# Row maxima turned by VectorE in four blocks, instead of by TensorE through PSUM

## The chip, the cores and the metric

One NeuronCore of a Trainium2 chip. The metric is the device time of one execution in microseconds; lower is better. Engines are named as in the profile: PE is TensorE (PEld its weight load), DVE is VectorE, ACT is ScalarE, POOL is GpSimd, SP is the engine whose queue issues nearly all DMAs.

## What is computed

One block of a diffusion transformer in float32: 16 batches of 256 tokens, width 256, 16 heads of 16. Self-attention with modulation and a gate, cross-attention to a context of 256 tokens, then an MLP of width 1024.

```python
x_norm = modulate(_ln(x), shift_a, scale_a)
q, k, v = split(x_norm @ W_qkv + b_qkv)
attn_w = softmax(einsum('bhqd,bhkd->bhqk', q, k) * scale)
x = x + gate_a[:, None] * (attn_out @ W_proj + b_proj)
q_c, (k_c, v_c) = _ln(x) @ W_qc + b_qc, split(_ln(context) @ W_kvc + b_kvc)
x = x + cross_attention(q_c, k_c, v_c) @ W_cproj + b_cproj
h = gelu(modulate(_ln(x), shift_m, scale_m) @ W_mlp1 + b_mlp1) @ W_mlp2 + b_mlp2
x = x + gate_m[:, None] * h
```

The softmax is taken against the exact maximum of each row of scores.

## The kernel before

The two attentions of 16 batches are 32 *units* n = 0 to 31, each one attention of one batch: s0 to s4, then alternating s5, c0, s6, c1 up to s15, c10, then c11 to c15 (s: self, c: cross). While unit n is computed, units ahead of it are prepared: n+1 has its scores for the maxima (`s`), n+2 its projections Q, K, V, n+3 its transposed, normalised input, n+4 its statistics. What is one step in the order of work for n is therefore mostly work of other units. In the loop, an even unit n from 2 to 22 has a self-attention unit at n+3 and a cross-attention unit at n+4; an odd one from 3 to 21 the other way round; from n = 23 on all that lie ahead are cross-attention.

Each unit has eight *beats* k = 0 to 7 (`beat(n, k)`). All engines and SP keep the program's order. In a beat, `visit(n, k)` first puts on PE four matmuls `s` (scores of unit n+1, rows on the partitions) and four matmuls `st` (scores of unit n, turned, with the negative maximum added through a 64th row of the operand). `s` has one PSUM buffer, which DVE reduces into `mx` (TENSOR_REDUCE) before the next beat's `s` may write it; `st` has one, which ACT turns into probabilities `pt` (`exp`) before the next `st`. After that each beat has its share of the rest: `o` (attention times values, `av_part`) in even beats, projections of n+2 and n+3 (`lanes`) in odd ones, input transposes (`psT`).

Q and K are kept in a stack `big` of 2 x 63 rows: high part, low part, high part (`h_q`, `l_q` and so on, sent by DMA from the projections), and in rows 63 and 127 the row maxima against a row of ones. `m_part(u, hf)` makes these rows for half `hf` of the heads: half 0 is complete after beat 3 of the unit before and used from beat 0 of unit u, half 1 complete after beat 7 and used from beat 4. PE transposes the 16 columns of `mx` into PSUM (`psm`), ACT negates them into `m`, SP sends `m` to the two rows. Half 0 stands in beat 4, half 1 in beat 0 of the unit itself.

Other names: `transposed(...).high` and `.low` make the high part `xTh` (ACT) and the remainder `xTl` (DVE for self-attention, in two pieces; for cross-attention ACT copies `y` and POOL subtracts) from one PSUM tile `psT`, in beat 3. `ln[0].steps[0]` are the statistics of a layer norm (`st_s`, `st_c`, DVE), `steps[1]` the aggregates `mv` and POOL's power `rs`, `steps[2]` POOL's application `xn`. For the attention's denominators, `pull` fetches sums `S` and outputs `U`, `recip` inverts S on DVE, `spread` writes S to DRAM (`rd`), `back` reads it back spread out as `R` (in beat 5), `norm` multiplies on POOL. The MLP follows the units and is not touched.

Of the kernel before, what the change touches and what calls it, by code (L numbers as in the profile page):

```python
# [21 lines left out]
def pixart_block(  # L22
# [56 lines left out]
    DVE.memset(wz, 0.0)  # L79
    ident = const.tile([P, P], F32, name="ident")  # L80
    make_identity(nc, ident)
    mhalf = const.tile([P, 2], F32, name="mhalf")
    POOL.memset(mhalf, -0.5)

# [1 line left out]
    vts = [const.tile([P, NT, NH, 32], F32, name=f"v{i}") for i in range(3)]  # L86
    wself = const.tile([P, 16, H], F32R, name="wself")
    ones = const.tile([8, N], F32, name="ones")
    DVE.memset(ones, 1.0)


    BMOD, BQKV, BQC, BKVC, BM1 = 0, 12, 18, 20, 24
# [246 lines left out]
    def transposed(src, name, scale=None, pool=False):  # L339

        o = Box()

        def place():
            o.ps = ps_gen(f"psT_{name}", SHORT)

        def turn(fs=range(KC)):
            if len(fs) == KC:
                place()
            for f in fs:
                for t in range(NT):  # L350
                    PE.transpose(o.ps[:, f * N + t * P:f * N + (t + 1) * P],
                                 src()[:, t, f * P:(f + 1) * P], ident)

        def high():
            hi = work.tile([P, KC, N], F32R, tag="xTh", name=f"xTh_{name}", bufs=4)
            lo = work.tile([P, KC, N], F32R, tag="xTl", name=f"xTl_{name}", bufs=4)
            o.xT = (hi, lo)
            if scale is None:
                ACT.copy(hi.rearrange("p k n -> p (k n)"), o.ps)
            else:  # L360
                for f in range(KC):
                    ACT.activation(hi[:, f], o.ps[:, f * N:(f + 1) * N], AF.Identity, scale=scale[f])

        def low():
            hi, lo = o.xT
            if scale is None:
                DVE.tensor_tensor(lo.rearrange("p k n -> p (k n)"), o.ps,
                                  hi.rearrange("p k n -> p (k n)"), ALU.subtract)
            else:
                for f in range(KC):  # L370
                    DVE.scalar_tensor_tensor(lo[:, f], o.ps[:, f * N:(f + 1) * N], scale[f],
                                             hi[:, f], ALU.mult, ALU.subtract)

        def full():
            o.y = work.tile([P, KC, N], F32, tag="y", name=f"y_{name}", bufs=1)
            if scale is None:
                ACT.copy(o.y.rearrange("p k n -> p (k n)"), o.ps)
            else:
                for f in range(KC):
                    ACT.activation(o.y[:, f], o.ps[:, f * N:(f + 1) * N], AF.Identity, scale=scale[f])  # L380

        def rest_pool():
            hi, lo = o.xT
            POOL.tensor_tensor(lo, o.y, hi, ALU.subtract)

        def low_pool():
            full()
            rest_pool()

        o.full, o.rest_pool, o.place = full, rest_pool, place  # L390
        o.parts = [turn, high, low]
        o.low_pool = low_pool
        o.turn, o.high, o.low = turn, high, low_pool if pool else low
        return o
# [245 lines left out]
    def s_tile(u, g, par, t, bank=None, home=sp):  # L640

        alone = bank is None
        if alone:
            turn_of_s[0] ^= 1
            bank = turn_of_s[0]
        apart = isinstance(home, tuple)
        for j in range(2):
            PE.matmul((home[bank] if apart else home[:, bank])[:, j * N:(j + 1) * N],  # L650
                      u.q[par * 64:par * 64 + 63, 2 * g + j, t * P:(t + 1) * P],
                      u.k[par * 64:par * 64 + 63, 2 * g + j, :], start=True, stop=True)
            if j == 0:
                yield
        if u.mx is None:
            u.mx = work.tile([P, 2, 2, 4, NT], F32, tag="mx", name=f"mx_{u.n}", bufs=3)
        mx = u.mx.rearrange("p f r a t -> p r f a t")
        a = slice(2 * (g % 2), 2 * (g % 2) + 2)
        if alone or apart:
            src = home[bank] if apart else sp[:, bank]  # L660
            DVE.tensor_reduce(mx[:, par, g // 2, a, t], src.rearrange("p (j n) -> p j n", j=2),
                              AX.X, ALU.max)
        elif bank == 1:
            DVE.tensor_reduce(mx[:, :, g // 2, a, t], home.rearrange("p r (j n) -> p r j n", j=2),
                              AX.X, ALU.max)
        yield

    def m_part(u, hf):

        pst = ps_gen(f"psm_{u.n}_{hf}", SHORT)  # L670
        PE.transpose(pst[:16, :P], u.mx[:, hf].rearrange("p r a t -> p (r a t)"), ident)
        m = work.tile([16, P], F32R, tag="m", name=f"m_{u.n}_{hf}", bufs=1)
        ACT.mul(m, pst[:16, :P], -1.0)
        SP.dma_start(u.q[63:P:64, 4 * hf:4 * hf + 4, :].bitcast(F32), m.bitcast(F32))

    def t_part(u, pair, par):

# [306 lines left out]
    def beat(n, k):  # L984
# [17 lines left out]
        if k == 4 and q2:  # L1002
            q2.Q.high()
            q2.Q.send_high()
        if k == 6:
            if q2 and not n:
                q2.V.keep()
            if p2 and not alone:
                p2.end()
        visit(n, k)  # L1010
        if k == 0:
            if cur:
                m_part(cur, 1)
            exps()
            if q3 and q3.ready:
                q3.T[0].place()
# [11 lines left out]
        elif k == 1:  # L1028
            exps()
            run(lanes(q2 and q2.Q, q2 and n and q2.V))  # L1030
            if prev:
                p1.pull(1)
            if lc:
                lc.ln[0].steps[0]()
            if lx:
                if lx.b in (0, B - 1):
                    lx.ln[1].steps[0]()
                lx.ln[1].steps[1]()
                lx.ln[1].steps[2]()
        elif k == 2:  # L1040
            exps()
            if cur:
                av_part(cur, 0)
            if q3:
                q3.T[0].turn((1,) if q3.ready else (0, 1))
            if ls:
                ls.ln[0].steps[0]()
            elif prev:
                p1.recip()
                p1.spread()  # L1050
            if not (q3 and q3.kind == "c"):
                spare(n)
        elif k == 3:
            if q3:
                q3.T[0].high()
                if q3.kind == "c":
                    q3.T[0].full()
            exps()
            if alone and p2:
                p2.proj(0)  # L1060
                p2.proj(1)
            elif n:
                run(lanes(p2, q2 and q2.Q))
            else:
                run(lanes(q2.V, q2.Q))
            if q3 and q3.kind == "s":
                q3.T[0].low()
            if prev and ls:
                p1.recip()
                p1.spread()  # L1070
        elif k == 4:
            if nxt and lx:
                m_part(nxt, 0)
            exps()
            if nxt and not lx:
                m_part(nxt, 0)
            if alone:
                p2.end()
            if cur:
                av_part(cur, 1)  # L1080
            if lx:
                lx.T[1].turn()
            if q2:
                q2.Q.low()
                q2.Q.send_low()
            if q3 and q3.kind == "c":
                q3.T[0].rest_pool()
                spare(n)
            if ls:
                ls.ln[0].steps[1]()  # L1090
                ls.ln[0].steps[2]()
                ls.ready = True
        elif k == 5:
            exps()
            run(lanes(q3 and q3.K, (None if alone else p2) if n else q2.V))
            if cur:
                o_out(cur, 0)
            if lc:
                lc.ln[0].steps[1]()
                lc.ln[0].steps[2]()  # L1100
                lc.ready = True
            v = unit(n + 5)
            if v and v.kind == "c":
                load(v)
            if prev:
                p1.back()
        elif k == 6:
            exps()
            if lx:
                lx.T[1].high()  # L1110
            if cur:
                cur.post.begin()
                av_part(cur, 2)
                cur.post.pull(0)
            if q3 and p2:
                q3.vk = lanes(q3.V, q3.K)
                run(q3.vk, 1)
            if p3:
                p3.store()
            if lx:  # L1120
                lx.T[1].full()
                lx.T[1].rest_pool()
        elif k == 7:
            exps()
            run(q3.vk if q3 and p2 else lanes(q3 and q3.V, q3 and q3.K))
            if late:
                p2.add()
                p2.added = True
            elif lc:
                lc.ln[1].steps[0]()  # L1130
            v = unit(n + 5)
            if v and v.kind == "s":
                load(v)
            if n == nu - 1:
                p2.add()
                p2.store()
# [99 lines left out]
```

## Time and profile before

| | |
|---|---|
| three runs | 748.71, 742.05, 743.37 us; median 743.37 |
| the profiled execution | 742.45 us, span of its trace 740.7 us |
| PE, DVE, ACT, POOL busy | 722.2, 569.4, 556.1, 528.5 us |
| granted clock of TensorE | 0.999 |
| DMA | 106.15 MB, mean 143 GB/s |

A row of a timeline gives the start in us from the span's beginning, the duration, the engine, the line (every operation goes through one helper, so all have L51), the operation, out<-in by the program's names, the shape, how many are merged (x4), and in brackets how long the engine was idle before it and what released it. SPq rows are DMAs being issued, not their transfer. A row of groups gives busy us, mean ns of one, and idle time before.

### The profile page before, as it was taken

How to read it: one execution, taken by the hardware profiler on the slowest of the kernel's cores; microseconds unless marked ns; L12 is line 12 of the kernel's file. 1: busy time of each engine (PE TensorE's matmuls, PEld its weight loads, DVE VectorE, ACT ScalarE, POOL GpSimd, SP SyncE). 2: the span in 40 equal slices, each digit the busy share in tenths (PEclk: the TensorE clock that was granted, in tenths of full speed). 3: DMA queues.
4: the chain of work that ended last, by engine and by line, in shares of the span. 5: the costliest groups of instructions: out<-in, count | busy, mean ns of one | idle time of the engine just before them, and what ended most of it. 6: DMA issues, size and time to landing. Idle time of an engine off the chain costs nothing.

```text
span 740.7 us, 22556 instructions
## 1 busy us (share of the span) xinstructions
PE 722.2 (98%) x9003; PEld 598.4 (81%) x9003; DVE 569.4 (77%) x882; ACT 556.1 (75%) x972; POOL 528.5 (71%) x525
## 2 busy tenths in 40 slices
PE   9999999999999999999999999999899999999997
PEld 8677777777777777777777787776479999999997
DVE  4778888878888887878788878778766877777762
ACT  5567888888888888887888888887766666666663
POOL 8465678797866868777686899985757676665663
PEclk9999999999999999999999999999999999999999
DMA  8365455544445455454555645545323132231311
GB/s 269 128 217 171 146 169 172 177 163 167 162 144 192 153 182 197 141 161 161 187 173 171 204 151 196 166 149 181 111 76 101 58 86 65 64 87 44 86 53 48
DMA packets 81388, 106.15 MB, mean 143 GB/s; under 512 B 16450, under 2 KB 44388, under 8 KB 81284
## 3 DMA queue, kind: packets, MB, share of 16 engines
q1 hardware_dynamic: 80180, 103.92, 43.3%
q8 instruction: 71, 1.16, 0.7%
q10 hardware_dynamic: 1104, 0.79, 0.4%
q14 instruction: 33, 0.27, 0.1%
HBM read 35.89 MB, written 8.98 MB: 61 GB/s over the span
## 4 chain that ended last, share of the span: by engine, by line
PE 92%; DVE 3%; ACT 2%; DMA 1%; issue 1%; POOL 1%; SPq 0%; ACTq 0%; POOLq 0%
PE s L51 18%; PE o L51 16%; PE st L51 14%; PE ph L51 13%; PE ps_P_s L51 4%; PE ps_k L51 3%; PE ps_v_s L51 3%; PE ps_kc L51 3%; PE ps_qc L51 3%; PE ps_v_c L51 2%; PE ps_q L51 2%; PE ps_P_c L51 2%; DVE mx L51 2%; PE psm L51 2%; PE psT_c L51 2%; PE psT_s L51 1%
## 5 line engine op out<-in xcount | busy, mean ns | idle before, releaser
L51 DVE TENSOR_REDUCE mx<-s 128x4 f32<-128x1024 f32 x252 | 307.7, 1221 | 89.2 <-PE s L51 88.7
L51 ACT ACTIVATE pt<-st 128x1024 f32<-128x1024 f32 x256 | 262.3, 1024 | 62.3 <-PE st L51 62.0
L51 PE MATMUL o<-pt,v 128*32 128x256 f32 x2048 | 137.1, 385 | 0.0
L51 PE MATMUL s<-big 63*128 63x256 f32 x1008 | 119.1, 307 | 5.5 <-DVE mx L51 4.0
L51 PE MATMUL st<-big 64*128 64x256 f32 (+1 forms) x1040 | 109.5, 284 | 3.1 <-ACT pt L51 1.7
L51 POOL TENSOR_TENSOR hl<-hf,hh 128x512 fp32r<-128x512 f32 x64 | 84.3, 1335 | 28.1 <-ACT hh L51 28.1
L51 PEld LDWEIGHTS s<-big 63*128 63x128 f32 x1008 | 79.0, 185 | 30.4 <-DVE mx L51 16.1
L51 PEld LDWEIGHTS st<-big 64*128 64x128 f32 (+1 forms) x1040 | 82.7, 186 | 6.6 <-ACT pt L51 3.4
L51 PEld LDWEIGHTS o<-pt,v 128*32 128x32 f32 x2048 | 53.4, 109 | 38.5
L51 ACT ACTIVATE hf<-ph,bT 128x256 f32<-128x256 f32 x120 | 50.4, 473 | 27.9 <-PE ph L51 27.9
L51 ACT ACTIVATE hh<-ph,bT 128x256 fp32r<-128x256 f32 x120 | 50.5, 472 | 20.9 <-PE st L51 9.8
L51 PE MATMUL ph<-wqch,wself 128*128 128x256 f32 x256 | 51.8, 286 | 1.3 <-ACT hh L51 1.3
L51 PE MATMUL ph<-wkch,wself 128*128 128x256 f32 x256 | 51.8, 286 | 0.0
L51 DVE TENSOR_SCALAR xn_m<-x,mv_m,rs_m 128x256 f32<-128x256 f32 x32 | 38.4, 1239 | 16.0 <-POOL rs_m L51 16.0
L51 PE MATMUL s<-big,hh 128*128 128x256 f32 x256 | 45.3, 276 | 0.0
L51 PE MATMUL st<-big,hh 128*128 128x256 f32 x256 | 45.0, 276 | 0.0
L51 PEld LDWEIGHTS ph<-wqch,wself 128*128 128x128 f32 x256 | 41.9, 191 | 1.9 <-ACT hh L51 1.5
L51 PEld LDWEIGHTS ph<-wkch,wself 128*128 128x128 f32 x256 | 41.9, 191 | 0.3
L51 POOL TENSOR_SCALAR xn_q<-x,mv_q,rs_q 128x256 f32<-128x256 f32 x32 | 38.9, 1225 | 1.7
L51 POOL TENSOR_SCALAR xn_c<-c,mv_c,rs_c 128x256 f32<-128x256 f32 x32 | 38.9, 1225 | 1.7
L51 PEld LDWEIGHTS s<-big,hh 128*128 128x128 f32 x256 | 38.8, 188 | 0.0
L51 PEld LDWEIGHTS st<-big,hh 128*128 128x128 f32 x256 | 38.8, 188 | 0.0
(214 smaller groups left out, 2215.7 us busy)
## 6 DMA issues: line engine op xcount, KB each, us to landing
big<-h_kc SPq DMA_DIRECT2D x32, 256.0 KB
big<-h_qc SPq DMA_DIRECT2D x32, 256.0 KB
big<-h_k SPq DMA_DIRECT2D x31, 256.0 KB
big<-h_q SPq DMA_DIRECT2D x31, 256.0 KB
big<-l_k SPq DMA_DIRECT2D x16, 256.0 KB
big<-l_q SPq DMA_DIRECT2D x16, 256.0 KB
g<-gd SPq DMA_DIRECT2D x16, 256.0 KB
U_s<-oT SPq DMA_DIRECT2D x32, 128.0 KB
```

The lines of the kernel that those rows point to most:

```text
L51: i = f(*a, **k)
```

## The change

`m_part` no longer uses PE, PSUM and ACT. `mx` becomes one of two constant tiles of 32 columns (both halves of a unit), used in turn; DVE transposes it in four blocks of 32 partitions x 32 columns into a tile of 32 partitions, and SP sends the 16 partitions of the half. The maximum stays positive, and the row of ones becomes one of -1. Half 0 is made at the start of beat 6, ahead of `visit`, half 1 at the end of beat 1. In beat 3 the remainder of a self-attention input is made half by DVE (`low_first`) and half by an ACT copy and a POOL subtraction (`low_second`). The statistics of a cross-attention context move from beat 1 to beat 2; those of a self-attention input already stood there.

```diff
-    DVE.memset(ones, 1.0)
+    DVE.memset(ones, -1.0)
...
+    maxima = [const.tile([P, 32], F32, name=f"mx{i}") for i in range(2)]
+    for t in maxima:
+        DVE.memset(t, 0.0)
...
+        def low_first():
+            hi, lo = o.xT
+            DVE.scalar_tensor_tensor(lo[:, 0], o.ps[:, :N], scale[0], hi[:, 0], ALU.mult, ALU.subtract)
+
+        def low_second():
+            hi, lo = o.xT
+            y = work.tile([P, KC, N], F32, tag="y", name=f"y_{name}", bufs=1)
+            ACT.activation(y[:, 1], o.ps[:, N:], AF.Identity, scale=scale[1])
+            POOL.tensor_tensor(lo[:, 1], y[:, 1], hi[:, 1], ALU.subtract)
...
-            u.mx = work.tile([P, 2, 2, 4, NT], F32, tag="mx", name=f"mx_{u.n}", bufs=3)
-        mx = u.mx.rearrange("p f r a t -> p r f a t")
+            u.mx = maxima[u.n % 2]
+        mx = u.mx.rearrange("p (f r a t) -> p r f a t", f=2, r=2, a=4)
...
     def m_part(u, hf):
-        pst = ps_gen(f"psm_{u.n}_{hf}", SHORT)
-        PE.transpose(pst[:16, :P], u.mx[:, hf].rearrange("p r a t -> p (r a t)"), ident)
-        m = work.tile([16, P], F32R, tag="m", name=f"m_{u.n}_{hf}", bufs=1)
-        ACT.mul(m, pst[:16, :P], -1.0)
-        SP.dma_start(u.q[63:P:64, 4 * hf:4 * hf + 4, :].bitcast(F32), m.bitcast(F32))
+        mT = work.tile([32, P], F32, tag="m", name=f"m_{u.n}_{hf}", bufs=1)
+        for c in range(0, P, 32):
+            DVE.transpose(mT[:, c:c + 32], u.mx[c:c + 32])
+        SP.dma_start(u.q[63:P:64, 4 * hf:4 * hf + 4, :].bitcast(F32), mT[16 * hf:16 * hf + 16])
...
         if k == 6:
+            if nxt:
+                m_part(nxt, 0)
...
         visit(n, k)
         if k == 0:
-            if cur:
-                m_part(cur, 1)
...
         elif k == 1:
-            if lc:
-                lc.ln[0].steps[0]()
...
+            m_part(cur, 1)
         elif k == 2:
...
-            if ls:
-                ls.ln[0].steps[0]()
-            elif prev:
+            if q4:
+                q4.ln[0].steps[0]()
+            if prev and not ls:
                 p1.recip()
                 p1.spread()
...
         elif k == 3:
...
             if q3 and q3.kind == "s":
-                q3.T[0].low()
+                q3.T[0].low_first()
+                q3.T[0].low_second()
...
         elif k == 4:
-            if nxt and lx:
-                m_part(nxt, 0)
             exps()
-            if nxt and not lx:
-                m_part(nxt, 0)
```

More of the change, by code (lines that the diff above doesn't have):

```diff
@@ L384, in rest_pool @@
             POOL.tensor_tensor(lo, o.y, hi, ALU.subtract)
+        def low_first():
[6 more added lines that the diff above has]
+            POOL.tensor_tensor(lo[:, 1], y[:, 1], hi[:, 1], ALU.subtract)
+        o.low_first, o.low_second = low_first, low_second
         def low_pool():
```

## The prediction

> **What bounds the kernel now.** I read the busy line of the page, its chain, and then the busy time by stretches, to see where the chain's engine has no air.
>
> ```profile
> PE 722.2 (98%) x9003; PEld 598.4 (81%) x9003; DVE 569.4 (77%) x882; ACT 556.1 (75%) x972; POOL 528.5 (71%) x525
> ...
> PE 92%; DVE 3%; ACT 2%; DMA 1%; issue 1%; POOL 1%; SPq 0%; ACTq 0%; POOLq 0%
> ...
> 200.00:300.00 100.00, 99.77 (x1456) 77.11 (x1453) 82.32 (x126) 83.12 (x132) 74.55 (x75) 1.00 0.50 167
> ...
> 500.00:540.00 40.00, 34.79 (x429) 23.89 (x426) 32.47 (x43) 29.63 (x43) 26.74 (x24) 1.00 0.42 135
> ```
>
> The columns of the last two are length, then PE, PEld, DVE, ACT, POOL. In the attention loop PE is busy 99.77 of 100 us and DVE and ACT 82 and 83: PE sets the pace, and work taken from it counts in full until another engine's queue is in the way. In the last attention units PE is busy only 34.79 of 40 us; I count no gain in units 29 to 31. PE's durations overlap, so I price by distances between starts, in one pair of units: 10 (an A unit: the unit three ahead is self-attention; there are 11, the even units 2 to 22) and 11 (a B unit: it is cross-attention; 16, the odd units 3 to 21 and 23 to 28).
>
> ```profile
> 195.79 0.40 PE L51 MATMUL st<-big 64*128 64x256 f32 x4
> 196.12 0.28 PE L51 MATMUL psm<-ident,mx 128*16 128x128 f32 x1
> 196.33 1.07 PE L51 MATMUL o<-pt,v 128*32 128x256 f32 x16
> ...
> 199.90 0.43 PE L51 MATMUL st<-big 64*128 64x256 f32 x4
> 200.26 1.07 PE L51 MATMUL o<-pt,v 128*32 128x256 f32 x16
> ...
> 203.81 0.45 PE L51 MATMUL st<-big 64*128 64x256 f32 x4
> ...
> 204.53 1.07 PE L51 MATMUL o<-pt,v 128*32 128x256 f32 x16
> ...
> 205.87 0.40 PE L51 MATMUL st<-big 64*128 64x256 f32 x4
> ...
> 211.55 0.40 PE L51 MATMUL st<-big 64*128 64x256 f32 x4
> ...
> 219.60 0.50 PE L51 MATMUL st<-big 64*128 64x256 f32 x4
> ...
> 220.24 1.07 PE L51 MATMUL o<-pt,v 128*32 128x256 f32 x16
> ...
> 227.73 0.41 PE L51 MATMUL st<-big 64*128 64x256 f32 x4
> ```
>
> These are beats 0, 2, 4 and 5 of unit 10, beats 0 and 4 of unit 11 and beat 0 of unit 12. From the start of st to that of o it is 0.36 us in beat 2, which has no psm between; 0.54 in beat 0, 0.72 in unit 10's beat 4 and 0.64 in unit 11's. So a transpose on PE costs 0.18 in beat 0, 0.36 in A's beat 4 and 0.28 in B's.
>
> **The change, part by part.** *The psm transposes go, with the negations.*
>
> ```profile
> L51 PE MATMUL psm<-ident,mx 128*16 128x128 f32 x64 | 17.6, 276 | 1.1
> ...
> L51 ACT ACTIVATE m<-psm 16x128 fp32r<-16x128 f32 x64 | 16.8, 262 | 3.5 <-PE psm L51 2.1 <-issue 1.2 <-ACT h_k L51 0.2
> ```
>
> Gross on PE: B units 0.18 + 0.28 = 0.46, by 16 = 7.4 us; A units 0.18 + 0.36 = 0.54, by 11 = 5.9 us. ACT's 16.8 us lie off the path (ACT is not the pacer) and I count them as nothing.
>
> *256 block transposes on DVE, four a half.* The trace has none. Bounds and cover:
>
> ```profile
> L51 DVE SCALAR_TENSOR_TENSOR bqkv<-st,bP x2: 192/192/192, 12.4 to 13.8; 128x32 f32<-128x32 f32 x2
> ...
> 199.39 0.74 DVE L51 BATCH_NORM_STATS2 st_c<-c 128x6 f32<-128x256 f32 x2
> 200.13 1.23 DVE L51 TENSOR_REDUCE mx<-s 128x4 f32<-128x1024 f32 x1
> 201.45 0.35 DVE L51 RECIPROCAL S_s<-S_s 128x32 f32<-128x32 f32 x1
> 202.18 1.22 DVE L51 TENSOR_REDUCE mx<-s 128x4 f32<-128x1024 f32 x1 [0.38 <-PE s L51]
> 203.32 0.87 DVE L51 SCALAR_TENSOR_TENSOR xTl_s<-psT_s,sc,xTh_s 128x256 fp32r<-128x256 f32 x2
> ...
> 207.22 0.24 DVE L51 BATCH_NORM_AGGREGATE mv_c<-st_c 128x2 f32<-128x6 f32 x2
> 208.11 1.23 DVE L51 TENSOR_REDUCE mx<-s 128x4 f32<-128x1024 f32 x1 [0.65 <-PE s L51]
> ...
> 215.90 1.22 DVE L51 TENSOR_REDUCE mx<-s 128x4 f32<-128x1024 f32 x1 [0.51 <-PE s L51]
> ...
> 224.27 1.22 DVE L51 TENSOR_REDUCE mx<-s 128x4 f32<-128x1024 f32 x1 [0.67 <-PE s L51]
> ```
>
> Low end 0.4 for four, if they follow each other as closely as the two aggregates (0.24 for two); high end 1.4, four reciprocals over as many elements. An ordinary operation on 32 elements a partition takes 0.192, four in a row 0.77; I take 0.7. In A's beat 1 they replace statistics of 0.74: even. At the end of beat 5 DVE idles 0.65 (A) and 0.67 (B), and in B's beat 1 0.51, waiting for PE's s; psm stands in beats 0 and 4, so these idle times stay. Being 0.2 late in B's beat 1 is within what the next s leaves. Not covered: units 3 and 28, which have 0.74 of statistics in the same beat (0.5 each), and about 0.5 in all in units 29 to 31. Together +1.5; none at the low end; the high end is the fourth rival. Without the cover all 64 groups would cost 45 us.
>
> *Half the remainder.* In beat 3 of an A unit DVE does one half (0.48 of 0.87), ACT copies the other (one activation more) and POOL subtracts it.
>
> ```profile
> 203.82 0.84 ACT L51 ACTIVATE h_qc<-ps_qc,bP 128x256 fp32r<-128x256 f32 x2 [0.33 <-PE ps_qc L51]
> 204.55 1.02 ACT L51 ACTIVATE pt<-st 128x1024 f32<-128x1024 f32 x1
> ...
> 207.55 0.23 POOL L51 TENSOR_SCALAR rs_c<-mv_c 128x2 f32<-128x2 f32 x1 [4.40 <-DVE mv_c L51]
> ```
>
> POOL's half lies in its 4.40 us of idleness: nothing. ACT's is not free. In the built program the copy waits for DVE's half (both read one PSUM tile), and queued behind it on ACT are h_qc, then exp, for which the next st waits (one st buffer). Worked out for unit 10, all 0.18 earlier after beat 0: the maximum of beat 2 starts at 199.95, the moved statistics and the reciprocal follow, so that of beat 3 starts at 202.05 (1.14 + 0.68 + 0.27 later; 0.05 lost), DVE's half ends at 203.2 + 0.48 = 203.7, ACT's copy at about 204.2 (0.47, half of h_qc's pair), h_qc starts there instead of 203.64, exp at 204.9, ending at 205.9. The st that stood at 205.87 and could have stood at 205.33 starts at 205.9: the 0.54 of the A unit is gone. So A units count 0. The bounds: +0.05, and -0.54 if the copy does not wait.
>
> *The sending.* Half 0's DMA used to be issued in beat 4, now after the transposes that end beat 5, and on SP's queue it has moved past l_q, the context load and `back` (R), before g, S and U. The first st of the next unit needs it.
>
> ```profile
> 191.75 0.65 SPq L51 DMA_DIRECT2D R_c<-rd_c  x1
> 195.97 1.28 POOL L51 TENSOR_TENSOR U_c<-U_c,R_c 128x512 f32<-128x512 f32 x1
> ...
> 207.70 0.66 SPq L51 DMA_DIRECT2D R_s<-rd_s  x1
> 211.85 1.28 POOL L51 TENSOR_TENSOR U_s<-U_s,R_s 128x512 f32<-128x512 f32 x1 [0.73 <-DMA R_s<-rd_s]
> ...
> 223.69 0.65 SPq L51 DMA_DIRECT2D R_c<-rd_c  x1
> 229.69 1.29 POOL L51 TENSOR_TENSOR U_c<-U_c,R_c 128x512 f32<-128x512 f32 x1 [1.74 <-DMA R_c<-rd_c]
> ...
> 552.11 0.56 SPq L51 DMA_DIRECT2D S_c<-oT  x1
> ...
> 553.98 0.35 DVE L51 RECIPROCAL S_c<-S_c 128x32 f32<-128x32 f32 x1 [0.85 <-DMA S_c<-oT]
> ```
>
> Low end: a small transfer with nothing before it takes 1.87 us (552.11 to 553.98); issued at 208.2 it lands at 210.1, before 211.55. High end: it lands only with the R in front of it. That of unit 10 is there at 211.85; R now goes out 0.4 earlier (0.65 of a DMA slot less before it, h_qc later), so in time. In B units R goes out 0.7 earlier and st 0.46 earlier, a net 0.24: unit 11's R, at 229.69, would be 1.96 - 0.24 = 1.7 late, unit 9's, there at 195.97 or sooner, is in time. Between 0 and 1.7 in B units I take 0.25, near the end in time: POOL's start is only the latest moment at which R can have landed. 16 x 0.25 = 4.0; A units 0. Half 1's DMA (after S and U of `pull(1)`, needed by beat 4) has some 3 us: nothing.
>
> **Sum.** Against the profiled execution's 742.45 us (span 740.7): -7.4 + 1.5 + 4.0 = -1.9, so 740.6. The median of the three runs shown is 743.37, this execution 0.1% under it; the forecast lies 0.4% under the median. I hold that a measurement here tells about 1% from no change, so this is no change that can be told.
>
> **Rivals.** *Clean gain.* The DMA is in time everywhere, half of A's gain survives and the transposes stay nearer their low end: -7.4 - 3.0 + 0.5 gives 732.6. For it: PE's 99.77 of 100, and idle DVE at the very places where the transposes stand. Against it: the wait of ACT's copy, which the program has.
>
> *Slower: half 0 always comes behind R.* Place: the first st of a unit, PE waiting with all its queue. Price: the middle of 0 and 1.7, 0.85 in B units, and 0.3 in A units (unit 10's R lands 0.3 behind the old st): 13.6 + 3.3 - 7.4 + 1.5 gives 753.5. It decides from 0.37 us a B unit on, where the 5.9 us are eaten. For it: POOL waits for R in units 10 and 12. Against it: R's landing for POOL is that of its last part. [...]
>
> *Slower: transposes at their high end.* 1.4 for four makes DVE late by 0.7 to 0.9 at each place, of which some 0.2 is slack: 1.2 in B, 1.0 in A units, 30 us: about 769. It decides from about 0.85 for four on.
>
> **How the numbers follow.** Forecast 0.44, clean gain 0.33, R 0.17, long transposes 0.06. Faster by over 1% (under 735.9) is the clean gain, 0.33; slower by over 1% (over 750.8) the two last, 0.23; within 1% the rest, 0.44. The forecast's own range is 736 to 749; to leave no more than 2 in 10 out it must reach to the clean gain with both its terms full (-7.4 - 5.9 + 0.5: 729.7) and to R's price: 729 to 754.
>
> **What would show it.** Right: groups of transposes of about 0.7 us in DVE's idle time with no new wait of s for mx; ACT's y_s waiting for DVE's xTl_s in even units, and st for pt behind it; B units about 0.46 shorter where the DMA is in time; a new wait of PE's st for big<-m in beat 0, about 0.25 on the mean. Wrong: A units half a microsecond shorter (then 732); that wait over 0.4 on the mean (then over 743); or s waiting for mx in beats 2 and 6 (long transposes).

## The result and the profile after

The changed kernel takes 764.66 us (median of 4 runs, 764.46 to 766.20) against 743.78 for the kernel before: ratio 1.0274, 95% interval 1.0223 to 1.0325. It is slower by 2.7%; the forecast was 740.6, with a range up to 754. The profiled execution has a span of 763.0 us against 740.7, 22.3 more. The medians below leave out three executions in a slower state of the chip (764.64 us in run 3, 771.87 in the second part of run 6, and 1693 in run 8, the one that was profiled there). First the page's busy line and the two lines of its chain, then one stretch of the windows view (columns as before; the third number from the end is the granted clock):

```profile
PE 727.3 (95%) x8939; PEld 599.4 (79%) x8939; DVE 609.8 (80%) x1127; ACT 553.4 (73%) x921; POOL 539.2 (71%) x538
...
PE 70%; DVE 11%; DMA 8%; ACT 3%; issue 3%; SPq 2%; POOL 1%; ACTq 0%; DVEq 0%; POOLq 0%
PE s L51 14%; PE st L51 13%; PE ph L51 12%; PE o L51 10%; DVE mx L51 7%; DMA big<-m 6%; SPq L51 2%; PE ps_qc L51 2%; PE ps_q L51 2%; PE ps_v_c L51 2%; DVE m L51 2%; PE ps_P_s L51 2%; PE ps_v_s L51 2%; PE ps_P_c L51 2%; PE ps_k L51 1%
...
200.00:300.00 100.00, 96.33 (x1396) 74.29 (x1398) 86.80 (x166) 79.78 (x120) 74.71 (x76) 1.00 0.49 164
```

In the loop PE was busy 99.77 of 100 us; now 96.33, and DVE went from 82.32 to 86.80. The chain shows where PE stands still: it was 92% PE, and now holds 11% DVE and 8% DMA, with `mx` and the transfer `big<-m` as its largest lines that are not PE. Two things thus hold PE up. The groups and waits views name them:

```profile
L51 DVE STREAM_TRANSPOSE m<-mx 32x32 f32<-32x32 f32 x256 | 50.1, 196 | 3.1
...
L51 PE MATMUL st<-big 64*128 64x256 f32 (+1 forms) x1040 | 112.6, 290 | 16.0 <-DMA big<-m 8.5 <-ACT pt L51 4.9 <-ACT h_k L51 0.8
...
L51 PEld LDWEIGHTS s<-big 63*128 63x128 f32 x1008 | 78.8, 186 | 41.2 <-DVE mx L51 29.2 <-issue 10.8 <-DVE mv_s L51 0.4
...
ACT y_s L51 <- DVE xTl_s L51: 5.8, 13, 0.5
```

The two groups of PE in the kernel before:

```profile
L51 PE MATMUL st<-big 64*128 64x256 f32 (+1 forms) x1040 | 109.5, 284 | 3.1 <-ACT pt L51 1.7
L51 PEld LDWEIGHTS s<-big 63*128 63x128 f32 x1008 | 79.0, 185 | 30.4 <-DVE mx L51 16.1
```

The idle time ahead of `st` went from 3.1 to 16.0 us, 8.5 of it waiting for the maxima; the wait of `s` for `mx` went from 16.1 to 29.2.

The same units 10 and 11 that the prediction priced: the first `st` of a unit now waits for its row of maxima, 0.95 us in the A unit 10 and 0.29 in the B unit 11; and the four transposes of unit 11 take 0.81 (beat 1) and 0.84 us (beat 5), not 0.7.

```profile
201.72 0.48 PE L51 MATMUL s<-big 63*128 63x256 f32 x4
203.15 0.51 PE L51 MATMUL st<-big 64*128 64x256 f32 x4 [0.95 <-DMA big<-m]
...
218.69 0.50 PE L51 MATMUL s<-big 63*128 63x256 f32 x4
219.49 0.51 PE L51 MATMUL st<-big 64*128 64x256 f32 x4 [0.29 <-DMA big<-m]
...
223.13 0.81 DVE L51 STREAM_TRANSPOSE m<-mx 32x32 f32<-32x32 f32 x4
...
231.20 0.84 DVE L51 STREAM_TRANSPOSE m<-mx 32x32 f32<-32x32 f32 x4
```

I measure a beat by the distance between the starts of PE's `s`. Beat 0 without a wait is 2.02 us long in this kernel (2.22 before). Over units 2 to 28, 20 of 27 first beats are longer than that by over 0.1, by 14.3 us in all, and A and B units alike (0.57 and 0.50 on the mean).

### The profile page after: what moved, and what is told of

It reads as the page before. It is cut to its first block, busy times and chain, and to the rows that moved or that the text cites. A ratio compares the mean times of both kernels' runs of the same rounds, so it can differ in the third digit from the quotient of the medians.

```text
span 763.0 us, 22640 instructions
## 1 busy us (share of the span) xinstructions
PE 727.3 (95%) x8939; PEld 599.4 (79%) x8939; DVE 609.8 (80%) x1127; ACT 553.4 (73%) x921; POOL 539.2 (71%) x538
## 4 chain that ended last, share of the span: by engine, by line
PE 70%; DVE 11%; DMA 8%; ACT 3%; issue 3%; SPq 2%; POOL 1%; ACTq 0%; DVEq 0%; POOLq 0%
PE s L51 14%; PE st L51 13%; PE ph L51 12%; PE o L51 10%; DVE mx L51 7%; DMA big<-m 6%; SPq L51 2%; PE ps_qc L51 2%; PE ps_q L51 2%; PE ps_v_c L51 2%; DVE m L51 2%; PE ps_P_s L51 2%; PE ps_v_s L51 2%; PE ps_P_c L51 2%; PE ps_k L51 1%
## 5 line engine op out<-in xcount | busy, mean ns | idle before, releaser
L51 PE MATMUL o<-pt,v 128*32 128x256 f32 x2048 | 139.6, 391 | 0.0
L51 PE MATMUL s<-big 63*128 63x256 f32 x1008 | 121.3, 312 | 11.7 <-DVE mx L51 9.2
L51 PE MATMUL st<-big 64*128 64x256 f32 (+1 forms) x1040 | 112.6, 290 | 16.0 <-DMA big<-m 8.5
L51 PEld LDWEIGHTS s<-big 63*128 63x128 f32 x1008 | 78.8, 186 | 41.2 <-DVE mx L51 29.2
L51 DVE STREAM_TRANSPOSE m<-mx 32x32 f32<-32x32 f32 x256 | 50.1, 196 | 3.1
L51 ACT COPY oT<-o 128x512 f32<-128x512 f32 x64 | 37.5, 586 | 3.1 <-PE o L51 3.1
```

What stands on the lines that cost most here:

```text
L51: i = f(*a, **k)
```

## The experiments

Theory 1: half 0 is late because R stands ahead of it. Theory 2: the four transposes are too long for DVE. Theory 3: ACT's copy eats the A units' gain. Theory 4: unit 0's half 1 stands behind the set-up's weight loads. All medians stand beside 743.5 for the kernel before.

**1. Half 0 ahead of R and of the context load.** In beat 6, behind `m_part(nxt, 0)`:

```diff
             if nxt:
                 m_part(nxt, 0)
+            v = unit(n + 5)
+            if v and v.kind == "c":
+                load(v)
+            if prev:
+                p1.back()
```

> The changed kernel, with the context load and R (back) moved behind half 0's DMA on SP's queue, so that half 0 goes first; nothing else differs. Theory 1 (half 0 is late because R and the load are ahead of it, in the queue or on the DMA engines): the first st of a unit no longer waits for big<-m, and most of the 15 us of beat 0 come back: 764.7 - 13 = about 752, less what R, now 0.7 us later, costs POOL. Rival (half 0 is late because the transposes stand at the end of beat 5 and any DMA from there comes too late): the wait stays, 762 to 766.

Measured 759.84 (ratio 1.0224, 1.0194 to 1.0254), where about 752 was expected. The wait is gone (the excess of the first beats is 0.7 us in one unit), but only 5 us come back: R, now behind the load in odd units, is late for POOL, whose `U_c` waits 27.0 us for it against 13.2 in the next run, and beats 2 and 3 of the A units grow from 3.92 to 4.24.

**2. Half 0 ahead of R alone** (the load stays in beat 5).

> As the one before, but only R (back) goes behind half 0's DMA; the context load (odd units) stays ahead of it. If R is what holds half 0 up: within 2 us of the one before (about 752 to 754). If it is the load: the even units gain, the odd ones don't: about 758. If neither: 762 to 766.

Measured 753.63 (1.0142, 1.0107 to 1.0177): 11 us come back, and no first beat is longer than 2.02 by over 0.1. SP's issues and the `st` of beats 7 and 0 at the start of unit 17, of the changed kernel and then of this one:

```profile
313.75 1.10 SPq L51 DMA_DIRECT2D R_s<-rd_s  x1
...
314.90 0.59 SPq L51 DMA_DIRECT2D big<-m  x1
316.57 0.40 PE L51 MATMUL st<-big 64*128 64x256 f32 x4
...
319.50 0.50 PE L51 MATMUL st<-big 64*128 64x256 f32 x4 [0.95 <-DMA big<-m]
```

```profile
313.29 0.58 SPq L51 DMA_DIRECT2D big<-m  x1
313.96 0.67 SPq L51 DMA_DIRECT2D R_s<-rd_s  x1
...
314.65 0.41 PE L51 MATMUL st<-big 64*128 64x256 f32 x4
...
316.48 0.40 PE L51 MATMUL st<-big 64*128 64x256 f32 x4
```

Behind R the 8 KB of maxima release the `st` 4.60 us after their issue began (314.90 to 319.50); the small transfer of the prediction, with nothing before it, took 1.87. Ahead of R the first `st` of unit 17 starts 3.19 us after the issue (313.29 to 316.48) and does not wait.

The trace also holds the moments at which each DMA's semaphore is counted up, which no view prints. Taken from the start of the issue to the last count, half 0 needs 1.79 to 1.92 us in the kernel before and 1.73 to 2.39 in this run, but 2.34 to 4.78 in the changed kernel (all of units 2 to 29). There its last count lies within 0.35 us of R's last count in 26 of the 28 units.

**3. The kernel before, with only half 0's DMA put behind R.** The maxima go through TensorE as ever; `m_part` keeps the DMA back, and beat 6 sends it.

> The kernel before with one thing of the change: half 0's DMA is issued in beat 6, behind the context load and R on SP's queue; the maxima are still turned by TensorE and negated by ACT in beats 0 and 4. Theory 1 alone from the other side (a place behind R costs the first st of each unit a wait of 0 to 1.5 us, 0.5 on the mean, in A and B units alike): 743.5 + 27 x 0.5 = about 757. Rival (the place behind R hurts only together with the transposes, which send the half out later): 743 to 747.

Measured 756.42 (1.0165, 1.0120 to 1.0209), 13.0 more than before where 13.5 was expected. This is theory 1 by itself, without any transpose on DVE.

**4. R issued from ACT's queue** at the same place of the changed kernel.

> The changed kernel with R issued from ACT's queue at the same place of the program (beat 5), so that half 0's DMA no longer stands behind it on SP's queue; nothing else differs. If it is SP's queue (its order alone) that delays half 0: the wait of st for big<-m vanishes in the units where R goes out in time, about 750 to 752 and what ACT's 0.6 us a unit costs. If it is the DMA engines, which have R's 256 KB in hand when half 0's 8 KB come: the waits stay, 764 or more.

Measured 763.23 (1.0267, 1.0235 to 1.0299). In units 2 to 28 the wait is less (10 first beats, 6.0 us; R now goes out up to 0.5 sooner) but not gone:

```profile
295.38 0.58 ACTq L51 DMA_DIRECT2D R_c<-rd_c  x1
...
296.95 0.57 SPq L51 DMA_DIRECT2D big<-m  x1
...
301.99 0.50 PE L51 MATMUL st<-big 64*128 64x256 f32 x4 [1.35 <-DMA big<-m]
```

SP issued the maxima with nothing of R on its queue, 1.57 us after R, and they came 5.04 us later. The context load `c` stands ahead of them on that queue, but by the counts it had landed at 298.96; R landed at 301.43 and the maxima at 301.85. Over units 2 to 29 half 0 lands 0.18 us behind R on the median. So the order on SP's queue does not explain it: the 8 KB land when R's 256 KB do, with R issued from ACT's queue (0.18 us behind) as from SP's (within 0.35 in 26 of 28 units). What ties the two landings together, no row here shows. In the changed kernel the semaphore of the R issued at 313.75 is first counted up at 315.31, then eight times from 317.30 to 319.65 (POOL's `U` starts at 319.72); that of half 0, issued at 314.90, first at 315.90, then at 319.31 and 319.37. The time is no better because this execution waited 5.0 us in unit 0 and 1.4 for another transfer.

**5. Also unit 0's half 1 in beat 0**, ahead of the weight loads, on top of run 2.

> The run with R (back) behind half 0's DMA, and besides it unit 0's half 1 turned and sent in beat 0, ahead of the set-up's weight loads, as the kernel before does; nothing else differs. Theory 4 (unit 0's half 1 waits behind weight loads that the set-up puts on SP's queue in beats 0 and 1 of unit 0): the long beat of unit 0 (7.1 and 3.6 us in beats 4 and 5) goes back to about 2 each: 753.6 - 5 = 748 to 749. Rival (the start varies from run to run for another cause): 752 to 755.

Measured 752.56 (1.0114, 1.0086 to 1.0141), where theory 4 had 748 to 749. Unit 0 falls from 22.8 us (of which 4.1 were one wait for `big<-m`) to 17.0 (17.3 in the kernel before); but the median falls by 1.1 only, since the end of this execution is 3.8 longer, and 1.1 is less than the two intervals can tell apart. The profiles of the other runs bear theory 4 out for unit 0 itself: in all six kernels that send its half 1 in beat 1 it takes 20.0 to 23.4 us, in the five that send it in beat 0 as one transfer 16.5 to 17.3 (19.9 and 18.5 in runs 9 and 10, with four pieces).

**6. One block transpose in place of four**, on top of run 5. This measures a price: three quarters of the maxima are left out.

```diff
-        for c in range(0, P, 32):
-            DVE.transpose(mT[:, c:c + 32], u.mx[c:c + 32])
+        DVE.transpose(mT[:, :32], u.mx[:32])
```

> The run just named (R behind half 0, unit 0's half 1 in beat 0) with one block transpose a half in place of four; three quarters of the subtracted maxima are zero, that part of the computation is left out. Theory 2 (with the DMA in time, it is the length of the four transposes that eats the gain on PE, in beat 1 as well as in beat 5): A units 15.97 to 15.65, B units 16.22 to 15.80, so 11 x 0.32 + 16 x 0.42 + 1 = 11 us less than the run just named: about 738, faster than before. Rival (DVE's other work or ACT's copy eats the gain, not the transposes): 746 to 749.

Measured 739.71 (0.9956, 0.9928 to 0.9984): 12.9 less than run 5, and 0.4% faster than before. What PE's weight load of `s` waits for, in run 5, in run 6 and in run 7:

```profile
L51 PEld LDWEIGHTS s<-big 63*128 63x128 f32 x1008 | 78.0, 185 | 41.7 <-DVE mx L51 31.3 <-issue 9.7 <-DVE l_qc L51 0.2
```

```profile
L51 PEld LDWEIGHTS s<-big 63*128 63x128 f32 x1008 | 78.3, 185 | 32.3 <-DVE mx L51 19.0 <-issue 12.6 <-DVE st_s L51 0.2
```

```profile
L51 DVE STREAM_TRANSPOSE wz<-wz 32x32 f32<-32x32 f32 x252 | 49.1, 195 | 4.8
...
L51 PEld LDWEIGHTS s<-big 63*128 63x128 f32 x1008 | 77.9, 185 | 34.0 <-DVE mx L51 21.7 <-issue 8.8 <-DVE l_q L51 1.5
```

31.3 us of waiting for DVE's maxima become 19.0. The same edit on the unchanged order of DMAs, which came first, gave less:

> The changed kernel with one block transpose a half in place of four: three quarters of the subtracted maxima are zero, that part of the computation is left out; the DMA has the same size. Theory 2 (the group of 0.85 us ends beat 5 late and delays the maximum of beat 6): -0.2 in each B unit's beat 6 (-3.3 us), -2 in unit 0, and half 0 is issued 0.6 us sooner. If half 0's landing hangs on its issue, beat 0's waits shrink by up to 0.6 in each unit, some 9 us more: about 750. If it hangs on R on the DMA engines (landing at a set time behind R), they stay: about 758.

Measured 759.55 (1.0219, 1.0175 to 1.0263), 5 less than the changed kernel. In the profiled execution, which at 765.01 was the longest of the four, beat 6 of the B units fell to 1.80, as expected, but the first beats' excess rose to 21.3 us in 24 units: what DVE no longer delayed now waited for the DMA.

**7. Four dead transposes a group on the kernel before**, with the statistics moved as in the change.

> The kernel before with the statistics moved to beat 2 as in the change, and four block transposes of a tile of zeros added on DVE at the ends of beats 1 and 5, whose result nobody uses; the maxima still go through TensorE. It prices the transposes alone, on top of the psm. The prediction's term (they lie in idle time, +1.5): 745. Theory 2 (0.85 a group is more than DVE's idle time there, about 0.2 us a group is not covered): 64 x 0.2 = 13, 755 to 758.

Measured 747.77 (1.0084, 1.0054 to 1.0113): +4.2, not 13. With the psm still on PE the transposes cost little (third of the three fences of run 6: 21.7 us of waiting for `mx`, 16.1 before). My expectation was wrong by the same mistake as the prediction, from the other side.

**8. The whole remainder on DVE**, on the changed kernel and then on run 5.

> The changed kernel with the whole remainder of the self units on DVE as before the change (low in place of low_first and low_second); nothing else differs. Theory 3 (ACT's copy y_s, which waits for DVE's half, eats what the A units save): beat 5 of the A units loses its 0.42 us, beat 4 gets back the 0.2 that it had gained: -0.2 to -0.5 in each of 11 units, 759 to 763. Rival (the copy doesn't set the end; DVE is the one short of time in the A units): DVE has 0.4 us more to do in beat 3 ahead of the maximum of beat 4, and the A units grow: 766 to 769.

> The run with R behind half 0 and unit 0's half 1 in beat 0 (752.6), with the whole remainder of the self units on DVE as before the change. Theory 3 in its first form (ACT's copy eats what the A units save): A units shorter by 0.3 to 0.5, 748 to 749. Rival (DVE is the one short of time in beats 3 to 5, so the 0.4 us that come back to it cost what the copy cost): 751 to 754.

Measured 765.41 (1.0289, 1.0229 to 1.0349) beside 764.66, and 750.67 (1.0100, 1.0056 to 1.0144, three executions) beside 752.56: no difference that these intervals can tell; both medians lie between the times that were expected with and without theory 3. In the profile of the first, beat 5 of the A units falls from 2.52 to 2.27 us, and beats 4, 6 and 7 grow by 0.22 together; beats 1 to 7 take 13.73 beside 13.74 (medians).

**9. One transpose over 128 partitions, four DMAs of 2 KB a half**, on top of run 5.

> The run with R behind half 0 and unit 0's half 1 in beat 0, with one block transpose over all 128 partitions a half (four blocks in one instruction, so the rows lie in four groups of 16 partitions) and four DMAs of 2 KB in place of one of 8 KB; computes everything. Theory 2 gives -11 us for the shorter transposes; against it stand three more issues on SP a half, some 0.57 us each: half 0's last piece goes out 0.6 sooner and 1.7 later than in the run with four transposes, so 1.1 later, and lands 0.4 before the first st needs it if a piece lands in 1.75 us: 738 to 742. Rival (the pieces or the queue behind them, R, S and U, come late): 745 to 755.

Measured 765.44 (1.0297, 1.0267 to 1.0326), a miss, beyond the rival's 755 too. The transpose is as cheap as hoped: a block transpose took 194 ns over 128 partitions here and 196 over 32 in the changed kernel. But each half now has three more issues on SP, and transfers come late: R for POOL, and the pieces for `st`. The groups view of this run with POOL's and PE's waits, then POOL's wait in run 5, where `st` waits for no maxima:

```profile
L51 DVE STREAM_TRANSPOSE m<-mx 128x32 f32<-128x32 f32 x64 | 12.4, 194 | 0.4
...
POOL U_s L51 <- DMA R_s<-rd_s: 21.9, 7, 3.8
PE st L51 <- DMA big<-m: 6.0, 8, 2.5
```

```profile
POOL U_s L51 <- DMA R_s<-rd_s: 15.5, 8, 2.4
```

How much of the 12.9 us each of these waits costs was not separated.

**10. A mixture meant to win**: half 0 by TensorE as before, half 1 by one such transpose and four pieces.

> A mixture meant to beat both: half 0 turned by TensorE in beat 4 and sent there, as before; half 1 turned by VectorE at the end of beat 1 with one block transpose over 128 partitions and sent as four pieces of 2 KB (unit 0: in beat 0); the whole remainder on DVE; the statistics as in the change; R in its old place. Theory 2: beats 0 and 1 together 4.07 where the kernel before has 4.18 and the run with four transposes 4.17: 27 x 0.11 = 3 us less than before, 740 to 741, if half 1's pieces, needed in beat 4, come in time. Rival (three more issues on SP a unit make other DMAs late): 746 to 755.

Measured 743.90 (1.0004, 0.9976 to 1.0032): the same as before, where 740 to 741 was expected. Beats 0 and 1 together did fall to 4.10 (4.18 before), but single waits for other transfers (beats of 3.56 and 3.42 us in units 1 and 23) took it back. No version that computes everything was found to beat the kernel before.

## Why the prediction was wrong

The spans can be set side by side from the starts of `s` at units 1, 28 and 30. Rows of PE's timeline of the kernel before, the changed one, run 2 and run 6:

```profile
51.88 0.51 PE L51 MATMUL s<-big 63*128 63x256 f32 x4 [1.06 <-DMA big<-l_q]
...
484.23 0.48 PE L51 MATMUL s<-big 63*128 63x256 f32 x4
...
516.49 0.50 PE L51 MATMUL s<-big 63*128 63x256 f32 x4 [1.09 <-DVE mx L51]
```

```profile
55.15 0.44 PE L51 MATMUL s<-big 63*128 63x256 f32 x4
...
501.40 0.45 PE L51 MATMUL s<-big 63*128 63x256 f32 x4
...
535.01 0.50 PE L51 MATMUL s<-big 63*128 63x256 f32 x4 [1.09 <-DVE mx L51]
```

```profile
58.51 0.41 PE L51 MATMUL s<-big 63*128 63x256 f32 x4
...
493.67 0.48 PE L51 MATMUL s<-big 63*128 63x256 f32 x4
```

```profile
50.86 0.51 PE L51 MATMUL s<-big 63*128 63x256 f32 x4 [0.20 <-DMA S_s<-oT]
...
477.75 0.47 PE L51 MATMUL s<-big 63*128 63x256 f32 x4
```

Units 1 to 27 take 432.3 us before, 446.3 after, 435.2 with R behind half 0, 426.9 with the short transpose as well (run 5 lies at 435.3, so the start does not enter). This gives the terms of the sum:

| term | predicted | measured |
|---|---|---|
| PE's gain, A units 0 | -7.4 | -5.4 (432.3 to 426.9, one short transpose a half still in it) |
| the length of the transposes | +1.5 | +8.4 (426.9 to 435.3) |
| half 0 behind R | +4.0 | +11.1 (435.2 to 446.3) |
| ahead of unit 1 and from unit 28 on | (0.5 of the 1.5) | +8.4 (3.3 + 1.3 + 3.8) |
| sum | -1.9 | about +22.4 (spans: 22.3) |

*PE's gain* was right in kind: in run 6 the B units fall from 16.20 to 15.88 us, the A units from 15.84 to 15.80, that is by nothing, as said.

*The sending* was booked 7.1 us too low. The wait was on record, as the rival that half 0 always comes behind R. The step that failed is the choice of 0.25 in B units "near the end in time" and of 0 in A units. I inferred R's landing from the moment at which POOL's `U` starts in three units, and took half 0 for early where R is early. By the semaphores' counts half 0 comes with R in both kinds of units (within 0.35 us in 26 of 28); R takes 3.5 to 5.9 us from its issue in the changed kernel, 4.65 on the median, and the first `st` is ready some 4.6 us after R's issue, so R's own variation decides which unit waits. The wait is 0.53 us on the mean (14.3 over 27), above the 0.4 that was named as a sign of being wrong. Of 14.3 us of waiting 11.1 are lost, for a late beat 0 gives DVE time to catch up: beat 1 then takes 2.02 where it takes 2.16 in run 2.

*The transposes* were booked some 7 us too low. They were mis-sized (0.81 to 0.84 for 0.7), but that is the smaller part. What failed is the sentence "psm stands in beats 0 and 4, so these idle times stay". DVE's idle time there was time in which it waited for PE (0.65, 0.51 and 0.67 us in the prediction's rows, each ended by PE's `s`). Taking psm from PE shortens that time, and the transposes want to lie in it: the sum booked the same half microsecond twice, as a gain on PE and as cover on DVE. Runs 6 and 7 show both halves: with psm in place the transposes cost 2.2 us in units 1 to 27 (434.5), nearly as forecast; with a short transpose PE's gain appears; without psm and with four transposes run 5 is 3.0 slower there than before. With four transposes it makes no gain whether psm is on PE (434.5) or not (435.3). The sign that was named for long transposes came: beat 6 of the B units takes 2.08 us where it took 1.83, with `s` waiting for `mx`. That rival put the deciding point at 0.85 for four, which is about where they are.

*ACT's copy* waits for DVE as predicted (5.8 us, 13 times), and the A units gain nothing, as predicted (15.80 for 15.84 in run 6). But taking the copy away does not bring the gain back while there are four transposes (run 8); what lengthens beats 4, 6 and 7 in its place was not traced. Without the copy and with short transposes nothing was run; with the copy and short transposes (run 6) beat 5 of the A units still takes 2.45 us, 2.11 before. So how much of the A units' gain the copy costs stays open.

*Start and end* were counted at half a microsecond. Of the 3.3 us ahead of unit 1, 2.7 stand in unit 0 (20.0 for 17.3), whose half 1 is sent a beat later than before; in run 5, which sends it in beat 0, they are gone (17.0). With four transposes a group, beats 2 and 6 of units 28 and 29 grow by some 0.4 to 0.7; this goes with the short transpose (run 6: 32.2 for units 28 and 29, 32.3 before). The 3.8 us from unit 30 on differ from execution to execution, as the last section tells.

## What to carry to other kernels

Idle time of an engine that waits for the bottleneck is not free cover for a change that shortens the bottleneck: book it once (here +8.4 us where +1.5 was booked). A small transfer that something waits for is worth trying ahead of a large one: here 8 KB behind 256 KB cost 11.1 us in units 1 to 27, and with the large one on another queue 6.0 us of the first beats' 14.3 stayed. To see when a transfer lands, look at its semaphore's counts or for its first reader, not for a reader that has other reasons to be late. An edit that shows little gain while another wait is in front of it (one transpose on the old order of DMAs, 5 of 13 us) should be tried again once that wait is gone.

## What the hardware showed beyond that

A block transpose took 195 to 196 ns for 32 x 32 and 194 for 128 x 32, and four of the former in a row took about four times that, 0.81 to 0.84, while the two aggregates of the prediction, of 0.16 each (median), follow each other within 0.24. What makes the one pair overlap and the four not was not tried.

In the changed kernel the granted clock was lower at the start and in the last units, where PE also stood still; it was 1.00 throughout in the profiled execution before. Windows of the changed kernel:

```profile
32.00:40.00 8.00, 6.88 (x53) 5.52 (x52) 7.23 (x12) 3.95 (x6) 3.84 (x7) 0.87 0.30 78
40.00:48.00 8.00, 7.23 (x72) 5.22 (x71) 4.58 (x6) 4.05 (x7) 1.53 (x2) 0.71 0.72 230
...
536.00:544.00 8.00, 6.92 (x68) 4.23 (x69) 5.37 (x9) 4.98 (x6) 5.51 (x5) 0.79 0.41 128
...
552.00:560.00 8.00, 6.52 (x54) 3.05 (x54) 5.20 (x7) 5.20 (x6) 6.20 (x6) 0.79 0.34 100
```

An estimate from these clocks: over the four stretches of 8 us PE lacks 3.4 us of clock at the start (8 x (0.13 + 0.29)) and 3.4 at the end (8 x (0.21 + 0.21)), about the size of the 3.3 and 3.8 us of the table's last row. Run 2 has such a stretch at its start only (0.57 from 48 to 56), run 5 at its end only (0.79 from 520 to 528 and from 536 to 544); from unit 30 on the changed kernel and run 5 take 228.0 and 228.4 us, the kernel before and run 2 224.2 and 224.6. What sets it off stays open, and with it how these microseconds divide between the standing still and the clock.
